# Turning 128-row blocks with VectorE squares of 32 and a DRAM store instead of PE transposes, in a cross-attention and coupled-FFN kernel

## The chip, the cores and the metric

The kernel runs as one program on one NeuronCore of a Trainium2 chip. The time is the device time of one execution in microseconds (us). The engines are named as in the profile: PE (TensorE matmul), PEld (TensorE weight load, which overlaps PE), DVE (VectorE), ACT (ScalarE), POOL (GpSimd) and SP (SyncE, which issues the DMAs here; SPq is its queue). Each engine works through its own instructions in order and waits on semaphores for the others.

## What is computed

`x` is (8, 1024, 512) in fp32, the context is (8, 64, 512). The reference, cut to what matters:

```python
x = x + xattn(layernorm(x), ctx, ctx, Wq, bq, Wk, bk, Wv, bv, Wo, bo, phase)   # 16 heads of 32
x = x + ffn(layernorm(x), ...)

# xattn
qh, kh = rotate(split(q @ Wq.T + bq), phase), rotate(split(k @ Wk.T + bk), phase)
attn = softmax(einsum('bhqd,bhkd->bhqk', qh, kh) / sqrt(32))
return merge(einsum('bhqk,bhkd->bhqd', attn, split(v @ Wv.T + bv))) @ Wo.T + bo

# ffn
gf = global_net(x.mean(axis=1, keepdims=True))
out = x
for _ in range(3):
    tf = sigmoid(gelu(gelu(gelu(out @ w1 + b1) @ w2 + b2) @ w3 + b3) @ w4 + b4)   # 512-512-256-128-1
    coupling = 0.1 + ar * (0.7 * gf + 0.3 * tf - 0.5) * 2.0
    out = out + coupling * twist(out)       # twist: the four quarters of a row, swapped and signed
return out
```

## The kernel before

**The planner.** The body writes nothing to the chip directly. Every call goes through `Engine` (line 304) and becomes an `Op` of a `Plan` (line 127) with an estimated cost (line 334), its dependencies and the buffers it needs. `schedule` (line 225) then plays these operations through as a list scheduler: at each moment every engine takes, of the operations that are ready and whose buffers fit, the one with the lowest priority number. That number is the place in the program plus hand-set offsets by stage (`SHIFT`, `LAST`; `TAIL` from the planned time `FINALE` on). The order found this way is the order in which each engine, and SP's queue of DMAs, runs on the chip. SBUF is cut into rooms: `ROOMS4` = 38 of 4 KB per partition (`r4`) and `ROOMS2` = 16 of 2 KB (`r2`); PSUM has 8 banks. `fits` (line 210) refuses a buffer beyond its tag's cap in `CAPS`, or, for the later operations, into the last `KEEP` rooms while early buffers are still to come.

**The work.** Each of the 8 batches is cut into two halves of 512 rows (`HB`, `TH` = 4 blocks of 128 rows), so there are 16 halves.

The first stretch is attention, half by half. `load_x` (line 472) loads the rows, `ln_stats` (line 680) and `normed` (line 692) form the layer norm, one ACT instruction per block of 128 rows (tile `xna`). The query product needs the 512 features on the partitions, so `turned` (line 704) turns the rows: 16 PE transposes of 128x128 per half into PSUM (`xp_a`), where each bank of 512 columns is then split into a high fp32r part (ACT cast) and a low part (DVE subtraction), `split`, line 438. The product is three fp32r matmuls per pair of blocks (`mm3`, line 428). POOL adds the output bias to the loaded rows meanwhile (line 743). `attn_half` (line 749) then runs the stages `q`, `m` (row maxima), `s` (scores, Exp), `pp` (denominators, which pass through DRAM: `rd`, `rb`), `av`, `o` (output product, added into the rows `xb` and stored as `x2d`) and `ln2`, whose normed rows `xnf` are stored in DRAM as `xnd`, row by row, and added up by POOL (`acc`).

The second stretch is the coupled FFN. A part is a half, except for the last two halves, which are cut into two parts each (`PARTS`). `ffn_load` (line 1019) loads a part's rows from `xnd` (tile `fxn`), and again turns them by PE transposes, 16 per half (`xp_f`), splits them into `fxT`, and forms and splits a sum of two quarters (`fs`). `ffn_part` (line 1048) computes the products K, A and B with first-layer weights that are combined beforehand, and then three cycles of the small network in `rest` (line 1081), in which the later cycles need no new first-layer product. The couplings come back per row through DRAM: `row_of` stores a row, `spread` loads it on all partitions, and `cc` is loaded with one element per descriptor (line 1217). `fin` combines and stores the output.

All GELUs wait for the last Exp (`last_exp`, line 920), and no FFN operation starts before the first PE operation of half `GATE` = 12 (line 931). The turning that the change touches, before:

```python
for t in range(len(piece)):
    with pl.group(also=d):
        pl.tensor.transpose(p[:, ts(t, P)], piece[t][i], ident)
split(d, i, p)
```

Of the kernel before, what the change touches and what calls it, by code (L numbers as in the profile page):

```python
# [22 lines left out]
P = 128  # L23
# [4 lines left out]
ROOMS4, ROOMS2 = 38, 16  # L28
GATE = 12
KEEP = 14  # L30
# [4 lines left out]
CAPS = {'xb': 8, 'wn': 5, 'bv': 1, 'bo': 1, 'jm': 1, 'rt': 1, 'kbd': 2, 'vbd': 2, 'pT': 8, 'acc': 2, 'w3': 3, 'w2f': 1, 'w3f': 1, 'h2': 12, 'w4': 1, 'gw2': 1, 'gw3': 1, 'fxn': 2, 'fs': 5, 'f1': 21, 'AB': 16, 'f2': 7, 'f3': 5, 'c': 12, 'x2': 6, 'xe': 13, 'aT': 6, 'wg': 6, 'w2': 2, 'h1': 8, 'xna': 14, 'xnf': 6, 'xT': 9, 'fxT': 14, 'p': 6, 'sp': 4, 'pp': 2, 'ap': 3, 'op': 2, 'qp': 3, 'xp': 1, 'K': 4, 'A': 6, 'B': 5, 'l2': 6, 'l3': 6, 'l4': 3, 'ct': 3, 'qf': 4, 'qr': 8, 'rb': 4, 'mT': 2, 'mw': 1, 'sT': 8, 'mp': 3, 'dn': 1}  # L35
PARTS = [1, 1, 1, 1, 1, 1, 1, 1, 1, 1, 1, 1, 1, 1, 2, 2]
LAST = {4: -100, 2: -280, 1: -280}
FINALE = 1140
TAIL = {('fin', 4): 354, ('c1', 6): 234, ('load', 3): -490, ('A', 3): -349, ('B', 3): -142, ('c0', 3): -372, ('c1', 3): -209, ('c2', 3): 222, ('fin', 3): -148, ('fin', 6): -215, ('c0', 1): -408, ('fin', 5): 375, ('fin', 1): -152, ('c0', 4): 32, ('load', 6): 78, ('A', 6): 10, ('B', 6): 93, ('c0', 6): -28, ('c2', 6): 61, ('B', 4): 35, ('c0', 2): 110, ('c2', 4): -161, ('c2', 5): 442, ('load', 1): -339, ('A', 1): 40, ('B', 1): 69, ('c1', 1): 114, ('c2', 1): 277, ('A', 2): -131, ('load', 4): 12, ('A', 5): 72, ('load', 5): -177, ('B', 5): 172, ('c0', 5): 88, ('c1', 5): -264, ('fin', 2): 410, ('load', 2): 81, ('c2', 2): 394, ('B', 2): 126, ('c1', 4): 94, ('c1', 2): 29, ('A', 4): -29}
SHIFT = {'ln1': 61, 'q': 194, 'm': 184, 's': -117, 'o': -42, 'pp': -69, 'av': 54, 'ln2': 112, 'load': -267, 'A': -154, 'B': -59, 'c0': -75, 'c1': 114, 'c2': 302, 'fin': -555}  # L40
# [26 lines left out]
class Buf:  # L67


    def __init__(self, make, shape, room=None, tag=None, cap=0):  # L70
        self.make, self.shape, self.room, self.tag, self.cap = make, shape, room, tag, cap
        self.ap = None
        self.writers, self.readers = {}, {}
        self.left = 0
        self.slot = None
        self.counted = False
# [50 lines left out]
class Plan:  # L127


    def __init__(self, tc):  # L130
        self.tc, self.nc, self.ops, self.items = tc, tc.nc, [], None
        self.rooms, self.pools, self.caps = {}, {}, {}
        self.gates, self.stage = [], (None, 0)

        self.late, self.early_bufs, self.keep = False, {}, {}
        for name in ("tensor", "vector", "scalar", "gpsimd", "sync"):
            setattr(self, name, Engine(self, name))
# [33 lines left out]
    def add(self, cost, items, also):  # L171
# [27 lines left out]
        op.late = self.late  # L199
# [10 lines left out]
    def fits(self, op):  # L210
# [4 lines left out]
        for room, bs in need.items():  # L215
            keep = min(op.keep.get(room, 0), self.early_bufs.get(room, 0))
            if len(self.rooms[room]) < len(bs) + keep:
                return False
            for b in bs:
                same = sum(o.tag == b.tag for o in bs)  # L220
                if self.caps[room, b.tag] + same > b.cap:
                    return False
        return True

    def schedule(self):
        ops = self.ops
        for op in ops:
            name, part = op.stage
            op.prio = op.n + SHIFT.get(name, 0) + LAST.get(part, 0)
            op.end_prio = op.prio + TAIL.get((name, part), 0)  # L230
# [5 lines left out]
        while done < len(ops):  # L236
            for e in engines:
# [8 lines left out]
                for o in can:  # L246
# [7 lines left out]
                    saving |= banks >= WIDE  # L254
# [3 lines left out]
                for b in op.bufs:  # L258
                    if b.slot is None:
                        b.slot = self.rooms[b.room].pop(0)  # L260
                        if b.counted:
# [42 lines left out]
class Engine:  # L304
# [3 lines left out]
    def __getattr__(self, method):  # L308
        def call(*args, **kw):
# [19 lines left out]
            issue.turn = method == "transpose"  # L329
# [4 lines left out]
    def cost(self, method, args, kw, outs, reads):  # L334
# [8 lines left out]
        if method == "transpose":  # L343
            return 0.109
# [25 lines left out]
def tile_xattn_ffn(  # L370
# [20 lines left out]
    pl = Plan(tc)  # L391
    pl.room("r4", rm, ROOMS4)
# [79 lines left out]
    def load_x(b, h):  # L472
        xb = []
        for j in range(2):
            t = t4([P, 2, D], "xb", f"xb_{b}_{h}_{j}")
            src = x[b, slice(h * HB + j * 2 * P, h * HB + (j + 1) * 2 * P), :]
            pl.sync.dma_start(out=t, in_=src.rearrange("(t p) d -> p t d", p=P))
            xb.append(t)
        return xb

# [27 lines left out]
    xb0 = load_x(0, 0)  # L508
# [164 lines left out]
    x2d, xnd = {}, {}  # L673
    for b in range(B):
        for h in range(NH):
            for d, nm in ((x2d, "x2d"), (xnd, "xnd")):
                t = dram.tile([P, TH, D], F32, name=f"{nm}_{b}_{h}")
                d[b, h] = pl.fixed(t, [P, TH, D], F32)
# [13 lines left out]
    def normed(src, st, tag, nm):  # L692
        mb, rs = st
        dst = []
        for t in range(TH):
            xn = t2([P, D], tag, f"{tag}_{nm}_{t}")
            pl.scalar.activation(
                xn, src[t // 2][:, t % 2, :], AF.Identity,
                bias=mb[:, t : t + 1], scale=rs[:, t : t + 1],
            )  # L700
            dst.append(xn)
        return dst

    def turned(pieces, tag, nm):


        r = []
        for j, piece in enumerate(pieces):
            w = len(piece) * P
            d = pair4([P, 2, w], tag, f"{tag}_{nm}_{j}")  # L710
            for i in range(2):
                p = bank([P, w], "xp", f"xp_{nm}_{j}{i}")
                for t in range(len(piece)):
                    with pl.group(also=d):
                        pl.tensor.transpose(p[:, ts(t, P)], piece[t][i], ident)
                split(d, i, p)
            r.append(d)
        return r
# [18 lines left out]
    def attn_qx(b, h, xb):  # L737
        nm = f"{b}_{h}"
        stage("ln1")
        xn = normed(xb, ln_stats(xb, f"a{nm}"), "xna", nm)  # L740
        for t in range(TH):
            v = xb[t // 2][:, t % 2, :]
            pl.gpsimd.tensor_tensor(v, v, bo_b, ALU.add)
        return turned(
            [[[xn[t][:, ts(2 * j + i, P)] for i in range(2)] for t in range(TH)] for j in range(2)],
            "xT", f"a{nm}",
        )

    def attn_half(b, h, xb, xnT):
# [49 lines left out]
        for k in range(2):  # L799
# [3 lines left out]
            with pl.group(cost=1.3, also=t):  # L803
# [7 lines left out]
                for g in range(4):  # L811
# [4 lines left out]
                    )  # L816
            for g in range(4):
# [57 lines left out]
        stage("o")  # L875
        for j in range(TH // 2):
# [13 lines left out]
        xn2 = normed(xb, ln_stats(xb, f"f{nm}", ln2[b, h]), "xnf", nm)  # L890
# [3 lines left out]
        acc = accs[b]  # L894
        for t in range(TH):
            pl.sync.dma_start(out=xnd[b, h][:, t, :], in_=xn2[t])
            pl.gpsimd.tensor_tensor(acc, acc, xn2[t], ALU.add)
# [7 lines left out]
    for i, (b, h) in enumerate(halves):  # L905
        starts[i] = len(pl.ops)
        stage()
        xb = load_x(b, h) if i else xb0
        xnT = attn_qx(b, h, xb)
# [9 lines left out]
        attn_half(b, h, xb, xnT)  # L919
# [12 lines left out]
    ORDER = ((4, 5), (2, 1), (0, 3))  # L932
# [4 lines left out]
    def ffn_weights():  # L937
# [3 lines left out]
        pl.vector.tensor_tensor(t[0][:, 0, :], W[2], W[0], ALU.subtract)  # L941
        pl.vector.tensor_tensor(t[0][:, 1, :], W[1], W[3], ALU.subtract)
# [76 lines left out]
    def ffn_load(b, h, t0, n):  # L1019
# [3 lines left out]
        xn = []  # L1023
        for j in range(n // 2):
            t = t4([P, 2, D], "fxn", f"fxn_{nm}_{j}")
            pl.sync.dma_start(out=t, in_=xnd[b, h][:, ts(t0 // 2 + j, 2), :])
            xn.append(t)

        H, L = range(2)
        xT = [two(n * P, "fxT", f"fxT_{nm}_{j}", F32R) for j in range(3)]  # L1030
        for i in range(2):
            s = t2([P, n * P], "fs", f"fs_{nm}_{i}")
            ps2 = []
            for k in (i, i + 2):
                p = bank([P, n * P], "xp", f"xp_f{nm}_{k}")
                j = next(j for j in (1, 2) if k in ORDER[j])
                q = ORDER[j].index(k)
                for t in range(n):
                    with pl.group(also=sum(xT, [])):
                        pl.tensor.transpose(p[:, ts(t, P)], xn[t // 2][:, t % 2, ts(k, P)], ident)  # L1040
                split(xT[j], q, p)
                ps2.append(p)
            pl.scalar.copy(s, ps2[0])
            pl.vector.tensor_tensor(s, ps2[1], s, ALU.add)
            split(xT[0], i, s)
        return xT

    def ffn_part(b, h, t0, n, xT):
# [3 lines left out]
        def product(tag, j, k):  # L1052
# [3 lines left out]
            for c in range(2):  # L1056
                mm3(
                    p, wH[:, c, ts(j, P)], wL[:, c, ts(j, P)], xH[:, c, :], xL[:, c, :],
                    c == 0, c == 1,
# [5 lines left out]
        h1 = two(W, "f1", f"f1_{nm}_0_")  # L1065
        for m in range(NC):
            pl.scalar.copy(Bt[m // 2][:, m % 2, :], product("K", m, 0))
        for m in range(NC):
            j, i = m // 2, m % 2
            p = product("A", m, 1)  # L1070
# [10 lines left out]
        def rest(cyc, h1):  # L1081
# [5 lines left out]
            for j in range(NC // 2):  # L1087
                if not plain:
                    hH, hL = two(W, "h1", f"h1_{nmc}_{j}", F32R)
                    pl.scalar.copy(hH, h1[j])  # L1090
                    low(hL, h1[j], hH)
                for i in range(2):
                    dc = 2 * j + i
                    for m in range(2):
                        if plain:
# [7 lines left out]
                            hH[:, i, :], hL[:, i, :], dc == 0, dc == NC - 1,  # L1103
# [5 lines left out]
            for dc in range(2):  # L1109
# [6 lines left out]
                pl.scalar.copy(hH, f2[:, dc, :])  # L1116
                low(hL, f2[:, dc, :], hH)
                mm3(p, w3p[0][:, dc, :], w3p[1][:, dc, :], hH, hL, dc == 0, dc == 1)
            gelu(f3, p, o3)
            rows = compact and (cyc < CYCLES - 1 or not 0 < part_from_last[0] <= DIRECT2)  # L1120
            if rows:
# [3 lines left out]
                c = small([P, P], "cs", f"c_{nmc}", 4)[: DK * n, :]  # L1125
# [10 lines left out]
            else:  # L1136
# [3 lines left out]
                with pl.group(also=(c,)):  # L1140
                    for t in range(n):
                        pl.tensor.matmul(
                            p[:, t : t + 1], lhsT=f3[:, ts(t, P)], rhs=bcol[:, ow4 : ow4 + 1],
# [46 lines left out]
        if compact:  # L1190
            al, be = (small([P, P], "abs", f"{k}s_{nm}", 4)[: DK * n, :] for k in ("al", "be"))
# [23 lines left out]
        for k, r in enumerate((al_r, be_r)):  # L1215
            with pl.group(cost=(0.5, 4.0)):
                pl.sync.dma_start(out=cc[:, k, :], in_=r.rearrange("o (t p) -> p (o t)", p=P))
# [102 lines left out]
```

## Time and profile before

| | |
|---|---|
| time, median of 3 runs (lowest, highest) | 1298.01 us (1296.53, 1298.63) |
| the profiled execution, its time | 1300.96 us |
| its span in the profile | 1299.1 us |
| mean granted TensorE clock | 0.991 |
| ACT busy | 851.7 us, 1482 instructions |
| POOL busy | 342.4 us, 427 instructions |
| DMA packets, bytes | 111106, 159.07 MB |

The profile is of one execution. Busy time is the time in which an engine had an instruction running; several may overlap, so the mean duration of one instruction times the count can exceed the busy time. A group line reads: engine, operation, output<-input by the program's tile names, shape, count | busy us, mean ns of one | idle time of the engine just before them, and what ended it. All operations have line L326, that of the helper that issues them, so the tile names tell them apart. The PE profile spaces matmuls more closely than their durations: a 128x512 matmul is listed with about 0.39 us and the next one starts 0.23 us later; what a matmul costs on PE's path is the distance from its start to the next one's start.

### The profile page before, as it was taken

To read this page: it belongs to the slowest core of one execution; us is meant where nothing else is said; L and a number is where in the kernel's file an instruction comes from. 1 tells how busy PE (TensorE), PEld (TensorE's weight loads), DVE (VectorE), ACT (ScalarE), POOL (GpSimd) and SP (SyncE) were. 2 spreads that over 40 slices of the span, in tenths; PEclk is the share of its full clock that TensorE was granted. 3 is DMA by queue.
4 is the path that set the end of the run, shared out by engine and by line. 5 is a ranking of instruction groups with operands and counts; after the bars stand their busy time and mean duration, and the time that the engine had idled before them with its cause. 6 is when DMAs were issued, how large, how long until landed. Compare 5 with 4: busy or idle time off the path is not lost. (4 is left out here: it accounts for less than half of the span.)

```text
span 1299.1 us, 21813 instructions
## 1 busy us (share of the span) xinstructions
PE 1264.9 (97%) x8083; PEld 973.9 (75%) x8083; DVE 1067.5 (82%) x1761; ACT 851.7 (66%) x1482; POOL 342.4 (26%) x427
## 2 busy tenths in 40 slices
PE   8999999999999999999999999999999999999995
PEld 7776677666776767666778877788778787789884
DVE  6757887778887878679578988999889898989995
ACT  4663455546455454535467888788787877878886
POOL 3501443424344333322101110111101221001264
PEclk9999999999999999999999999999999999999997
DMA  6313443343434434264213325443244432532444
GB/s 241 108 35 108 159 135 101 128 100 131 109 130 124 148 110 131 99 195 148 96 51 114 101 79 155 150 123 124 79 145 140 152 118 55 171 123 75 133 136 138
DMA packets 111106, 159.07 MB, mean 122 GB/s; under 512 B 33180, under 2 KB 58008, under 8 KB 111000
## 3 DMA queue, kind: packets, MB, share of 16 engines
q1 hardware_dynamic: 111000, 157.69, 38.7%
q8 instruction: 63, 1.03, 0.3%
q14 instruction: 43, 0.35, 0.1%
HBM read 105.62 MB, written 52.03 MB: 121 GB/s over the span
## 5 line engine op out<-in xcount | busy, mean ns | idle before, releaser
L326 PE MATMUL l<-h,w2H 128*128 128x512 f32 (+1 forms) x832 | 247.6, 381 | 2.4 <-ACT h L326 1.2
L326 PEld LDWEIGHTS l<-h,w2H 128*128 128x128 f32 x832 | 148.1, 190 | 32.2 <-issue 4.6
L326 PE MATMUL l<-h,w2L 128*128 128x512 f32 (+1 forms) x416 | 155.0, 373 | 0.0
L326 POOL TENSOR_TENSOR pc<-cc,rs 128x4 f32<-128x4 f32 (+1 forms) x18 | 14.4, 803 | 518.1 <-DMA cc<-ber 515.7
L326 ACT ACTIVATE f<-l,bcol 128x512 f32<-128x512 f32 (+1 forms) x162 | 100.6, 640 | 56.9 <-PE l L326 53.6
L326 DVE TENSOR_TENSOR h<-f,h 128x1024 fp32r<-128x1024 f32 x84 | 102.0, 1218 | 8.2 <-ACT h L326 7.3
L326 POOL TENSOR_TENSOR xb<-xb,bo_b 128x512 f32<-128x512 f32 x64 | 89.8, 1425 | 37.0 <-ACT xna L326 35.4
L326 POOL TENSOR_TENSOR acc<-acc,xnf 128x512 f32<-128x512 f32 x64 | 88.4, 1382 | 37.9 <-ACT xnf L326 34.1
L326 DVE TENSOR_REDUCE mw<-sp 128x8 f32<-128x512 f32 x128 | 82.6, 684 | 14.5 <-PE sp L326 14.3
L326 PEld LDWEIGHTS l<-h,w2L 128*128 128x128 f32 x416 | 79.0, 190 | 14.0
L326 ACT CAST h<-f 128x1024 fp32r<-128x1024 f32 x84 | 87.7, 1053 | 2.5 <-DVE h L326 1.0
L326 ACT ACTIVATE pT<-sT 128x512 f32<-128x512 f32 x128 | 66.2, 602 | 29.5 <-PE sT L326 22.4
L326 ACT ACTIVATE xna<-xb,mb_a,rs_a 128x512 f32<-128x512 f32 x64 | 48.1, 808 | 53.9 <-DVE mb_a L326 45.3
L326 ACT ACTIVATE f<-f,bcol 128x512 f32<-128x512 f32 x112 | 77.6, 727 | 5.0 <-DVE f L326 4.7
L326 ACT ACTIVATE xt<-xt,fa 128x256 f32<-128x256 f32 x128 | 65.0, 591 | 18.0 <-DVE fa L326 17.9
L326 DVE TENSOR_TENSOR xb<-op,xb 128x512 f32<-128x512 f32 x64 | 44.0, 687 | 34.7 <-PE op L326 34.7
L326 ACT ACTIVATE qf<-qp,bqr 128x512 f32<-128x512 f32 x64 | 42.5, 691 | 45.0 <-PE qp L326 44.9
L326 POOL TENSOR_TENSOR rs<-rs,mhalf 128x4 f32<-128x4 f32 x16 | 19.2, 1203 | 189.9 <-DVE rs L326 189.3
L326 DVE TENSOR_TENSOR f<-f,A 128x1024 f32<-128x1024 f32 x56 | 67.8, 1217 | 0.0
L326 ACT ACTIVATE xnf<-xb,mb,rs 128x512 f32<-128x512 f32 x64 | 48.2, 809 | 20.0 <-DVE mb L326 15.8
L326 DVE TENSOR_SCALAR pT<-pT 128x1024 f32<-128x1024 f32 x64 | 45.1, 713 | 19.4 <-ACT pT L326 19.3
L326 POOL TENSOR_TENSOR rs_a<-rs_a,mhalf 128x4 f32<-128x4 f32 x16 | 16.6, 1041 | 152.4 <-DVE rs_a L326 152.4
(402 smaller groups left out, 3646.0 us busy)
## 6 DMA issues: line engine op xcount, KB each, us to landing
xb<-in_x_dram SPq DMA_DIRECT2D x32, 512.0 KB
rb<-rd SPq DMA_DIRECT2D x128, 128.0 KB
x2d<-xb SPq DMA_DIRECT2D x32, 512.0 KB
xnd<-xnf SPq DMA_DIRECT2D x64, 256.0 KB
fxn<-xnd SPq DMA_DIRECT2D x32, 512.0 KB
x<-x2d SPq DMA_DIRECT2D x32, 512.0 KB
xt<-x2d SPq DMA_DIRECT2D x64, 256.0 KB
out_dram<-x SPq DMA_DIRECT2D x32, 512.0 KB
```

The lines of the kernel that those rows point to most:

```text
L326: f(*map(real, args), **{k: real(a) for k, a in kw.items()})
```

## The change

The rows are no longer turned by PE.

For the query product, `load_turned` loads a half's rows so that partition p holds rows 4p to 4p+3 (tile `xa`), the layer norm is written back in place, and the new `turned` lets DVE transpose each pair of blocks in squares of 32x32 into a tile `u` (tag `tn`, 8 KB per partition, one of two rooms `r8`). Four DMAs, one for each 32 partitions, then store `u` to DRAM as rows of the turned matrix (`xtd`); the 512 bytes that belong together are 32 rows times 4. Two DMAs load it back (`xf`), and it is split in pieces of 1024 columns. The rows for the residual are loaded a second time in stage `o`, after the first score product of that half, and POOL's bias addition moves there.

For the FFN, `turned` stores the second layer norm's rows in the same way in `xnd`, and `ffn_load` loads the part's turned matrix and splits it. In the halves of two parts the pieces are 256 bytes and there are eight stores. The columns of a part now stand in the order of (row in block, block), so the per-row couplings `cc` and `c2` are read as `(p t)`.

The planner is altered with it: rooms, caps and offsets are others, `KEEP` goes from 14 to 67, a new rule (`OWED`) keeps rooms of `r4` and `r2` free for operations of up to four units before, `NEAR` gives offsets for the first, the last attention halves and the last three FFN parts, and a wide PSUM group holds banks back only while too few are free. Several groups of operations now claim their output buffers earlier (`also`), and each product A waits for the planned copy of K with the same number.

The diff, cut to its core:

```diff
-ROOMS4, ROOMS2 = 38, 16
+ROOMS8, ROOMS4, ROOMS2 = 2, 35, 14
-KEEP = 14
+KEEP = 67
+OWED = (3, 0)
...
+            if room in ("r4", "r2") and left < OWED[op.late]:
+                owed = sum(self.open[room][max(0, op.unit - 4) : op.unit])
+                if left < min(OWED[op.late], owed):
+                    return False
...
+            op.prio += NEAR.get((name, op.unit), 0)
...
-                    saving |= banks >= WIDE
+                    saving |= banks >= WIDE and banks > len(self.rooms["bank"])
...
+    def load_turned(b, h):
+
+        return load_x(b, h, "xa", "(p t) d -> p t d", t=TH)
...
+    def turned(xn, d, nm, n=TH):
+
+
+        u = pl.tile("r8", [P, NC * NC, TH // n, DK, n], F32, "tn", f"tn_{nm}", ROOMS8)
+        for k in range(TH // 2):
+            to = u[:, :, 2 * k // n, :, 2 * k % n : 2 * k % n + 2]
+            pl.vector.transpose(
+                to.rearrange("p f k t -> p t f k"),
+                xn[k].rearrange("p t (f k) -> p t f k", k=DK),
+            )
+        for i in range(NC):
+            for k in range(TH // n):
+                at = slice((k * P + i * DK) * n, (k * P + i * DK + DK) * n)
+
+                def rows_(a, at=at):
+                    return d[1].rearrange("(f k) t -> k f t", k=DK)[:, :, at]
+
+                with pl.group(cost=(0.6, 2.0)):
+                    pl.sync.dma_start(
+                        out=d[0][:, :, at].via(rows_),
+                        in_=u[ts(i, DK), :, k, :, :].rearrange("p f k t -> p f (k t)"),
+                    )
...
+        normed(xa, xa, ln_stats(xa, f"a{nm}"))
+        turned(xa, xtd[b, h], f"a{nm}")
+        r = []
+        for j in range(2):
+            d = pair4([P, 2, HB], "xT", f"xT_{nm}_{j}")
+            t = t4([P, 2, HB], "xf", f"xf_{nm}_{j}")
+            with pl.group(cost=(1.5, 2.0), also=d):
+                pl.sync.dma_start(out=t, in_=xtd[b, h][0][:, ts(j, 2), :])
+            pl.scalar.copy(d[0], t)
+            low(d[1], t, d[0])
+            r.append(d)
+        return r
...
         stage("o")
+
+        pl.gates.append(scored)
+        xb = load_x(b, h, "xb", "(t p) d -> p t d", p=P)
+        pl.gates.pop()
+        for t in range(TH):
+            v = xb[t // 2][:, t % 2, :]
+            pl.gpsimd.tensor_tensor(v, v, bo_b, ALU.add)
...
+        turned(xn2, xnd[b, h], f"f{nm}", TH // PARTS[NH * b + h])
         for t in range(TH):
-            pl.sync.dma_start(out=xnd[b, h][:, t, :], in_=xn2[t])
-            pl.gpsimd.tensor_tensor(acc, acc, xn2[t], ALU.add)
+            pl.gpsimd.tensor_tensor(acc, acc, xn2[t // 2][:, t % 2, :], ALU.add)
...
-                for t in range(n):
-                    with pl.group(also=sum(xT, [])):
-                        pl.tensor.transpose(p[:, ts(t, P)], xn[t // 2][:, t % 2, ts(k, P)], ident)
-                split(xT[j], q, p)
-                ps2.append(p)
-            pl.scalar.copy(s, ps2[0])
-            pl.vector.tensor_tensor(s, ps2[1], s, ALU.add)
-            split(xT[0], i, s)
+        xf_ = pl.tile("r8", [P, 4, W], F32, "fxn", f"fxn_{nm}", ROOMS8)
+        xf = [xf_[:, ts(j, 2), :] for j in range(2)]
+        for j, q in ((0, slice(1, 3)), (1, slice(0, NC, 3))):
+            with pl.group(cost=(1.5, 2.0), also=sum(xT, [])):
+                pl.sync.dma_start(out=xf[j], in_=xnd[b, h][0][:, q, t0 * P : t0 * P + W])
+            pl.scalar.copy(xT[1 + j][0], xf[j])
+            low(xT[1 + j][1], xf[j], xT[1 + j][0])
+        s = two(W, "fs", f"fs_{nm}_")[0]
         for i in range(2):
+            pl.vector.tensor_tensor(s[:, i, :], xf[1][:, i, :], xf[0][:, 1 - i, :], ALU.add)
+        pl.scalar.copy(xT[0][0], s)
+        low(xT[0][1], s, xT[0][0])
...
-                pl.sync.dma_start(out=cc[:, k, :], in_=r.rearrange("o (t p) -> p (o t)", p=P))
+                pl.sync.dma_start(out=cc[:, k, :], in_=r.rearrange("o (p t) -> p (o t)", p=P))
```

## The prediction

> **What bounds the kernel now.** I read, in this order: the engine totals and the 40 slices, PE's waits, the busy time per half in both stretches, the group lines of what is removed and of what resembles the new work, and PE's and SP's timelines.
>
> ```profile
> span 1299.1 us, 21813 instructions
> PE 1264.9 (97%) x8083; PEld 973.9 (75%) x8083; DVE 1067.5 (82%) x1761; ACT 851.7 (66%) x1482; POOL 342.4 (26%) x427
> PE   8999999999999999999999999999999999999995
> DVE  6757887778887878679578988999889898989995
> ```
>
> PE is busy 97% of the span and idle for 34 us in all, mostly at the two ends. DVE stands second, at 82%. PE's longest waits inside are small:
>
> ```profile
> PE sp L326 <- DVE qr L326: 7.6, 8, 1.4
> PE tr_cT L326 <- DMA c_n<-in_ctx_dram: 6.1, 2, 4.7
> PE l L326 <- DVE h_0L L326: 3.3, 3, 2.5
> ```
>
> (us in total, times, longest.) So PE's own list of instructions is the time, and DVE is what PE waits for where it waits at all. Four windows of busy time, two of attention (one half each, from the first query matmul of a half to the next half's) and two of the FFN:
>
> ```profile
> core 0: us, PE busy (x) PEld busy (x) DVE busy (x) ACT busy (x) POOL busy (x), PEclk, DMA share, GB/s
> 292.40:328.20 35.80, 34.99 (x272) 24.46 (x271) 28.55 (x52) 21.32 (x36) 18.98 (x16) 1.00 0.43 146
> 328.20:361.90 33.70, 33.70 (x270) 24.73 (x269) 26.71 (x49) 14.30 (x25) 9.43 (x6) 1.00 0.40 103
> 830.60:879.10 48.50, 48.50 (x252) 38.14 (x251) 41.66 (x59) 40.26 (x69) 5.13 (x12) 1.00 0.41 131
> 952.70:993.00 40.30, 40.30 (x204) 32.26 (x202) 36.03 (x50) 33.17 (x57) 5.17 (x12) 1.00 0.46 144
> ```
>
> An attention half takes 34.75 us on average of the two, with 27.6 us of DVE (79%); in the FFN DVE stands at 86% to 89% while PE is never idle. PE can thus be kept full beside a DVE at 89%.
>
> **Removed from PE.** 512 transposes: 256 of `xp_a` and 256 of `xp_f`.
>
> ```profile
> L326 PE MATMUL xp_a<-ident,xna 128*128 128x128 f32 x256 | 50.5, 274 | 0.0
> 314.62 1.95 PE L326 MATMUL dn<-pT,dsel 128*32 128x128 f32 x64
> 316.50 0.66 PE L326 MATMUL xp_a<-ident,xna 128*128 128x128 f32 x4
> 316.91 0.48 PE L326 MATMUL qp<-xT_a_1H,wq_1H 128*128 128x512 f32 x1
> 317.23 0.39 PE L326 MATMUL qp<-xT_a_1L,wq_1H 128*128 128x512 f32 x1
> 317.46 0.39 PE L326 MATMUL qp<-xT_a_1H,wq_1L 128*128 128x512 f32 x1
> ```
>
> The listed 274 ns overlap. On the path, four transposes take from 316.50 to 316.91, 0.41 us, and the first matmul after them holds the next back by 0.32 instead of 0.23 us: 0.50 us for a lone group of four. 128 groups of four then cost 128 x 0.41 = 52 us where the switch is paid anyway and 128 x 0.50 = 64 us where each group stands alone. Many stand alone or even in ones and twos; I take 60 us, 30 in each stretch. All of it is on the path, since PE is full around them. No PE instruction is added.
>
> **Moved to DVE.** 2 transposes per turn, 2 turns per half: 64, each 128x1024 fp32 from SBUF to SBUF, written with a step of 16 bytes. No row of before shows this operation. The nearest rows of that size:
>
> ```profile
> L326 DVE TENSOR_TENSOR h<-f,h 128x1024 fp32r<-128x1024 f32 x84 | 102.0, 1218 | 8.2 <-ACT h L326 7.3 <-PE B_3p L326 0.3
> L326 DVE CAST qr<-qf 128x1024 fp32r<-128x1024 f32 x32 | 25.8, 805 | 19.3 <-ACT qf L326 19.1
> L326 DVE RECIPROCAL rc<-dn 128x128 f32<-128x128 f32 x16 | 15.2, 948 | 6.0 <-PE dn L326 6.0
> ```
>
> Below: the cast, 0.81 us. Above: the reciprocal's rate, 948 ns for 128, would make 7.6 us of 1024. The transpose only moves data, which is near the first two; I take the slower of them, 1.22 us: 64 x 1.22 = 78 us. DVE saves where 512-wide low parts from PSUM become 1024-wide ones: for the queries 64 x 0.68 = 43.6 us become 32 x 1.22 = 39; for the FFN 67.6 us (the four `fxT` groups, 38.4 + 19.2 + 6.7 + 3.3) become about 48 x 1.22 = 58.6. Net 78 - 14 = +64: DVE 1131 us.
>
> Beside PE that lies as follows. An attention half has 16 transposes less, 30/16 = 1.9 us: PE's period goes to 32.9. DVE's goes to 27.6 + 4 x 1.22 - 0.3 = 32.2, 98% of it. That looks like a tie, but busy time counts the tails between dependent instructions: four reductions back to back take 2.48 us at 294.40 in DVE's timeline, 0.62 each, where one alone is listed with 0.68. With 9% off, DVE needs about 29.5 of 32.9 us, 90%. An FFN part loses 1.9 us of PE from about 40 and 0.6 of DVE from 36: 93%. So PE remains the bound with less cover; I give 4 us back for DVE waits in attention, none in the FFN. At the lower end, 0.81, that give-back goes; at the upper, 7.6, DVE alone would need 1067 - 14 + 486 = 1539 us.
>
> One rule speaks against this step. The Trainium skill, "SBUF — State Buffer", on SBUF's 16-byte cachelines, wants two hits on a line for full rate, though it calls a step of four fp32 elements free; the transpose's step is just four, and each element it writes lies in a line of its own. No row here has such a write. If the rate halved, the sum by this rule would be about that of the second rival below; by the plain row it is the forecast.
>
> **DMA and SP.** Added: the store of `xtd`, its load and the second load of x, 16 halves x 3 x 1.05 MB = 50 MB.
>
> ```profile
> q1 hardware_dynamic: 111000, 157.69, 38.7%
> ```
>
> By bytes that is 38.7% x 50/157.7 = +12%. By packets: a turn is 2048 pieces of 512 bytes, 32,768 for the queries and 32,768 instead of 8,192 for `xnd`, with 16,000 or so for the loads some 74,000 more, +26% at this mean price. Either way, 51% to 65%, the engines are not full. The one-element packets of `cc` and `c2` shrink to a quarter or half, which I cost at nothing: POOL waits for them off the path. The Trainium skill, "DMA: Bandwidth & Descriptors", Specifications, says that pieces under 512 bytes are read, modified and written. The halves in one part just meet it; the two halves of two parts do not, with 4,096 pieces of 256 bytes each. No row here prices that, and by the rule the last halves' loads would come late and cost a few us.
>
> SP gets 4 + 2 + 2 issues per half more, and 8 for the two cut halves: 136. At the 0.3 to 0.6 us that its timeline shows per issue, about 61 us beside some 300 us of issue time; not a bound. New waits do stand in its queue: the stores wait for DVE, the loads for the stores. Behind them stand `rd` and `rb` (for `av`), `x2d`, and later x loads. The store and load of `c0` show the round trip:
>
> ```profile
> 675.47 0.51 SPq L326 DMA_DIRECT2D c0r<-c  x1
> 677.19 0.33 SPq L326 DMA_DIRECT2D c<-c0r  x1
> 680.34 2.37 DVE L326 TENSOR_TENSOR f<-B,c 128x1024 f32<-128x1024 f32 x2 [0.29 <-DMA c<-c0r]
> ```
>
> 1.72 us from store to the load's issue, 3.15 more to its use. A turn is then 2 x 1.22 on DVE, 4 x 0.45 issues, 1.7 landing, 2 x 0.45 issues, 3.1, and 1.05 + 1.22 for the split: 12 us from normed rows to the operand, where PE did it in 2. The query turn depends on x alone, so it can run a half (33 us) ahead; `xnd` went through DRAM already. I cost both at nothing. If that cover is gone, see the third rival. At the start nothing lies ahead: normed rows of half 0 feed transposes from 33.98 us on, the first query matmul starts at 47.76, and a 12 us turn fits just about; 3 us for that.
>
> The second load of x is released a score product early and needed at `o`; the whole of `av` lies between, so nothing. ACT loses the PSUM copies of `fs` and half of its cast starts, some 30 us off the path. The planner's new numbers I cannot price; -10 to +10 us for the order's luck, zero taken.
>
> **Sum.** Profiled execution 1300.96 (span 1299.1 and 1.9 around it) - 60 (PE) + 4 (DVE waits) + 3 (start) = 1248. The median is 2.95 below the profiled execution, so 1245; with the transposes at 64 instead of 60 it is 1241. I say 1243. Own range: 52 to 64 us of PE, 0 to 15 of waits, 10 either way for the order; all low ends together give 1298 - 64 + 3 - 10 = 1227, and all high ends but the order's 1298 - 52 + 15 + 3 = 1264.
>
> **Rivals.** Second: DVE becomes attention's bound. With t per transpose a half needs 27.3 + 4t of DVE; it reaches the old period of 34.75 at t = 1.86 us. The attention gain is then gone and the FFN's 30 us remain: 1298 - 30 = 1268. For it: 98% by plain busy time, and the unknown write step. Against it: the 0.62 us back to back, and that only one operand is read.
>
> Third, on the slower side: the turn through DRAM is not ahead, because the two 8 KB rooms and SP's order hold it back until shortly before its use. Its place is before the query product. If half of its 12 us show in each half, 16 x 6 = 96 us against 60 gained: 1298 - 60 + 96 = 1334. It decides from 60/16 = 3.75 us shown per half. For it: SP waits in order, and each turn needs a room until its stores have landed. Against it: a room is held some 6 us twice per 33 us, and PE has the previous half's `sT`, `dn`, `ap` and `op` to do.
>
> Fourth: transposes were filler in gaps that stay, and the order gives nothing: 1298. Against it: PE idles 0.8 us or less in the two attention windows, which leaves no such gaps. Fifth: the freed bank and the new order also win back some of the 34 idle us: 1218.
>
> **How the numbers follow.** Forecast 0.66; DVE-bound attention 0.15; turn exposed 0.10; nothing 0.03; order wins more 0.06. Two per mille, 2.6 us, is about what a measurement of this kernel tells from no change. Faster takes the first, second and fifth: 0.87; same 0.03; slower 0.10. The range reaches from the fifth's side, 1222, into the second, 1274; left out are the third and fourth and the tails, about 2 in 10.
>
> **What would show it.** No `xp` groups, PE busy near 1205 us and idle under 45. DVE near 1130 us, its transposes near 1.2 us; above 1.9 the second rival holds. PE's waits on `xT` for the query product, near zero if the turn is ahead. Wrong altogether if PE's busy time does not fall by 50 us, or if DVE's or DMA's waits on PE grow by more than it falls.

## The result and the profile after

The changed kernel takes 1352.55 us (median of 4 runs, 1348.44 to 1357.01), the kernel before 1298.32 us beside it: ratio 1.0421, 95% interval 1.0386 to 1.0456. It is slower by 54.6 us; the forecast was 1243. In what follows a difference to the kernel before is always (ratio - 1) x 1298 us, since the runs of before differ by 1 to 2 us from chip to chip.

The top of the page after, to be read against the lines of before in the prediction (engine totals, then busy tenths of PE, DVE and of the DMA engines in 40 slices, then the DMA queue):

```profile
span 1346.7 us, 20903 instructions
PE 1245.6 (92%) x7571; PEld 931.6 (69%) x7571; DVE 1168.6 (87%) x1739; ACT 828.5 (62%) x1360; POOL 343.8 (26%) x427
...
PE   8889888988999999998899999999999999989984
...
DVE  7699989988998898888978998699889899697895
...
DMA  6677778686866555556521432334253333441354
...
q1 hardware_dynamic: 175704, 208.03, 51.1%
```

PE has 512 instructions less, but its busy time fell by 19 us, not 60, and it is now idle for 101 us (span minus busy) instead of 34. Part of this is the granted clock, 0.973 after and 0.991 before: (1 - 0.973) x 1347 = 36 us of full clock are missing over the span, against (1 - 0.991) x 1299 = 12. An estimate from these figures is that the lower clock accounts for at most 25 us of the loss; it was not measured by itself, and it stands inside the costs found below rather than beside them, since PE's idle stretches come with them. DVE gained 101 us, not 64. The DMA share of the span came out at 51.1%, as forecast by bytes; the slices show what that mean hides: 6 to 8 tenths in the first half of the span, 3 to 4 in the second.

The new operation, from the groups by line:

```profile
L343 DVE STREAM_TRANSPOSE tn_a<-xa 128x1024 f32<-128x1024 f32 x32 | 64.6, 2033 | 0.5 <-ACT xa L343 0.3
L343 DVE STREAM_TRANSPOSE tn_f<-xnf 128x1024 f32<-128x1024 f32 x32 | 62.4, 1968 | 4.8 <-ACT xnf L343 4.5
```

2.03 and 1.97 us each, against 1.22 in the forecast and 1.86, from which on the second rival was to hold. The busy times per stretch of the attention, of after and of before:

```profile
core 0: us, PE busy (x) PEld busy (x) DVE busy (x) ACT busy (x) POOL busy (x), PEclk, DMA share, GB/s
60.00:150.00 90.00, 79.35 (x596) 52.00 (x596) 83.89 (x131) 48.29 (x74) 21.84 (x18) 0.94 0.76 224
150.00:300.00 150.00, 134.04 (x927) 90.81 (x928) 140.27 (x217) 71.39 (x108) 63.71 (x45) 0.98 0.74 215
300.00:450.00 150.00, 139.07 (x1027) 93.61 (x1025) 136.24 (x202) 72.73 (x110) 54.55 (x41) 0.98 0.67 193
```

```profile
60.00:150.00 90.00, 90.00 (x730) 64.93 (x729) 63.91 (x109) 43.06 (x72) 21.90 (x17) 1.00 0.27 82
150.00:300.00 150.00, 147.43 (x1162) 103.73 (x1160) 118.34 (x211) 79.04 (x129) 63.47 (x50) 1.00 0.43 128
300.00:450.00 150.00, 148.34 (x1135) 106.77 (x1127) 122.04 (x221) 75.10 (x123) 57.03 (x44) 1.00 0.40 121
```

In attention DVE is now the fuller engine (140 of 150 us) and the DMA engines carry 215 instead of 128 GB/s. PE's waits, the longest first and then those on the turned operand:

```profile
PE l L343 <- ACT h_0H L343: 10.4, 5, 5.4
PE mp L343 <- DVE mw L343: 7.6, 15, 1.8
PE dn L343 <- DVE pT L343: 7.3, 5, 3.6
PE sp L343 <- DVE qr L343: 6.9, 7, 2.1
...
PE qp L343 <- ACT xT_1H L343: 2.7, 2, 1.5
PE qp L343 <- DVE xT_1L L343: 2.0, 3, 0.8
```

The query turn runs ahead as forecast: PE waits for it 4.7 us in all. It waits for the rest of the attention's DVE work instead (`mw`, `pT`, `qr`). By the traces' start and end times of the named products:

| us | last output product (`op`) ends | first `A` of the FFN starts | end | from first `A` to end |
|---|---|---|---|---|
| before | 642 | 595 | 1299 | 705 |
| after | 666 | 645 | 1347 | 702 |

So there are two things to explain: attention lost 24 us (by its last product) to 50 us (by the FFN's first) where it should have gained 30, and the FFN, which has none of the query turn's DMAs and only the last two of the 64 transposes on its DVE, gained 3 us where it should have gained 30.

### The profile page after: what moved, and what is told of

It reads as the page before. It is cut to its first block, busy times and chain, and to the rows that moved or that the text cites. A ratio compares the mean times of both kernels' runs of the same rounds, so it can differ in the third digit from the quotient of the medians.

```text
span 1346.7 us, 20903 instructions
## 1 busy us (share of the span) xinstructions
PE 1245.6 (92%) x7571; PEld 931.6 (69%) x7571; DVE 1168.6 (87%) x1739; ACT 828.5 (62%) x1360; POOL 343.8 (26%) x427
## 3 DMA queue, kind: packets, MB, share of 16 engines
q1 hardware_dynamic: 175704, 208.03, 51.1%
## 5 line engine op out<-in xcount | busy, mean ns | idle before, releaser
L343 PEld LDWEIGHTS l<-h,w2H 128*128 128x128 f32 x832 | 151.8, 191 | 43.5 <-DVE h L343 11.3
L343 POOL TENSOR_TENSOR xb<-xb,bo_b 128x512 f32<-128x512 f32 x64 | 97.2, 1549 | 178.0 <-DMA xb<-in_x_dram 115.6
L343 POOL TENSOR_TENSOR pc<-cc,rs 128x4 f32<-128x4 f32 (+1 forms) x18 | 11.4, 634 | 442.1 <-DMA cc<-ber 307.3
L343 ACT ACTIVATE xa<-xa,mb_a,rs_a 128x512 f32<-128x512 f32 x64 | 47.7, 807 | 42.5 <-DVE mb_a L343 40.4
L343 DVE STREAM_TRANSPOSE tn_f<-xnf 128x1024 f32<-128x1024 f32 x32 | 62.4, 1968 | 4.8 <-ACT xnf L343 4.5
L343 DVE STREAM_TRANSPOSE tn_a<-xa 128x1024 f32<-128x1024 f32 x32 | 64.6, 2033 | 0.5 <-ACT xa L343 0.3
L343 ACT CAST xT_1H<-xf 128x1024 fp32r<-128x1024 f32 x16 | 16.8, 1048 | 64.7 <-DMA xf<-xtd 64.7
```

Source lines behind the costliest of these rows:

```text
L343: f(*map(real, args), **{k: real(a) for k, a in kw.items()})
```

## The experiments

In all of them each engine runs the same list in the same order as the kernel they come from (after, or before); only what an instruction does or moves is changed, or whether it is issued at all. The exceptions are the doubled transposes of e12 and DMAs that are added or cut in two.

**e1, dense writes.** The transposes write their 1024 elements one after another instead of with a step of four; the DMAs stay, so rows land in a scrambled order.

```diff
-            to = u[:, :, 2 * k // n, :, 2 * k % n : 2 * k % n + 2]
+            flat = u.rearrange("p f q k t -> p (f q k t)")[:, ts(k, 2 * D)]
+            to = flat.rearrange("p (t f k) -> p t f k", t=2, k=DK)
```

> The changed kernel with its order of instructions unchanged; DVE's transposes write their squares one after the other in SBUF (a step of 4 bytes) instead of with a step of 16 bytes, so the turned rows are arranged wrongly, while stores, loads and all else move the same bytes. Theory 1 (the write step makes a transpose 2.03 us instead of 1.2, and DVE is attention's bound): transposes near 1.2 us, DVE busy falls by 64 x 0.8 = 51 us, most of it on the path, time 1295 to 1310. Theory 2 (the turn through DRAM and its 512-byte pieces is late): 1340 to 1355 although the transposes are shorter. Theory 3 (the planned order itself is bad, whatever a transpose costs): also 1335 to 1355.

1337.04 us, ratio 1.0306 (1.0275 to 1.0336), and a transpose now takes 1231 ns. The write step costs 0.80 us of 2.03 per transpose and 15 us of the 54.6 by itself.

**e3, copies.** The same with a plain copy in place of each transpose.

> The changed kernel in the same order with a plain DVE copy of 128x1024 in place of each transpose, so that the rows are not turned. Theory 1: a copy takes 0.6 to 0.8 us, DVE falls by 64 x 1.3 = 83 us; if DVE still bound attention with 1.2 us, the time falls further than with dense writes, to 1270 to 1290; if not, it stays within 5 us of that run. Theories 2 and 3: 1335 to 1355.

1333.41 us, 1.0278 (1.0249 to 1.0306). A copy of `xa` takes 0.80 us, of `xnf` 1.24, where the dense transposes of e1 take 1.23 each. Moving the data is most of a dense transpose, and 4 us separate the two kernels, within their intervals.

**e2 and e9, a step of two elements, all rows in place.** If a half's rows are dealt in pairs, the transpose writes two adjacent elements (step 8 bytes). In e2 the load of x does the dealing:

```diff
+        src = x[b, ts(h, HB), :].rearrange("(i j k t) d -> j i k (t d)", i=NC, j=2, t=2)
```

> The same computation as the changed kernel, the same order and the same 512-byte stores; rows are loaded so that each transpose writes its pairs of rows side by side, with a step of 8 bytes. Theory 1: as the transposes of the two cut halves, which have this step and take 1.2 us; time 1295 to 1310. Theories 2 and 3: 1335 to 1355. If the step must be 4 bytes for the full rate, transposes stay near 2.0 us and the time near 1350.

1440.79 us, 1.1121 (1.1077 to 1.1164), though its transposes take 1.24 us. DVE's waits for the loaded rows show why, in e2 and then in after:

```profile
DVE st_a L343 <- DMA xa<-in_x_dram: 77.2, 17, 11.2
...
DVE st_a L343 <- DMA xa<-in_x_dram: 6.8, 6, 3.3
```

The load's outermost dimension is 4 here. The Trainium skill, "DMA: Bandwidth & Descriptors", section "Why a DMA increments its semaphore by 16 and not by 1", says that a DMA is spread over the largest number of engines up to 16 that divides its outermost dimensions, which makes four of this one; this run shows the late loads but not the engines. e9 keeps 128 partitions outermost, loads 4 KB runs and lets PE read the moving operand in the dealt order:

```diff
+            t = t4([P, 2, D], "xa", f"xa_{b}_{h}_{j}")
+            r = slice(h * HB + j * 2 * P, h * HB + (j + 1) * 2 * P)
+            pl.sync.dma_start(out=t, in_=x[b, r, :].rearrange("(p t) d -> p t d", t=2))
...
+        return v.via(lambda a: a.rearrange("p (i q w) -> p q i w", i=NC, q=2))
```

> The same computation as the changed kernel, in the same order and with the same stores: x is again loaded in whole runs of 4 KB per partition, DVE writes pairs side by side (a step of 8 bytes), and PE reads the columns of its moving operand in blocks of 64 to put them in natural order. Theory 1: transposes at 1.2 us as in the two cut halves, and a time like that of the run with dense writes, 1333 to 1342. If it stands near 1440 as the earlier run with pairs did, it was not the load of x in that run that cost 100 us. Theory 3 adds nothing here: the rest over 1298 stays.

1334.59 us, 1.0268 (1.0215 to 1.0320). The line of its query transposes (those of the FFN take 1237 ns):

```profile
L343 DVE STREAM_TRANSPOSE tn_a<-xa 128x1024 f32<-128x1024 f32 x32 | 39.5, 1234 | 0.6 <-ACT xa L343 0.5
```

So the load carries the e2 loss: all of it lies in attention (from first `A` to end e2 takes 702 us and e9 703), and the small loads of the couplings, which differ too, belong to the FFN. Two adjacent elements per write are as fast as dense ones, and the whole change with that repair is still 35 us slower than before.

**e4, bigger pieces.** The stores of the turn leave 8 KB in one piece instead of 16 of 512 bytes (the turned rows land in another order).

```diff
+                    return d[1].rearrange("(i k f) t -> i k (f t)", i=NC, k=DK)[at.start // P]
```

> The changed kernel in the same order and with its transposes as they are, but each store of a turn writes one run of 8 KB per partition instead of sixteen pieces of 512 bytes, so the turned rows stand in other places in DRAM. Theory 2 (small pieces load the DMA engines so that turns and other transfers come late): DMA share in attention falls from 0.7 towards 0.6, time 1300 to 1330. Theories 1 and 3: 1345 to 1355, unchanged.

1338.87 us, 1.0320 (1.0283 to 1.0356): 13 us of the loss go with the pieces, at the same bytes, with 118,104 packets instead of 175,704. The DMA share did not fall as expected: 0.76 from 150 to 300 us and 0.64 from 300 to 450, after 0.74 and 0.67.

**e5 and e6, a light turn.** e5 stores and loads only a fraction of the query turn's bytes; e6 in addition loads an eighth of the second x.

```diff
+                f = 1 if i and nm[0] == "a" else NC * NC
+                cut = lambda a, f=f: a[:, 0:f, :]
...
+                part = lambda a: a[:, :, 0:64]
+                pl.sync.dma_start(out=t.via(part), in_=xtd[b, h][0][:, ts(j, 2), :].via(part))
```

> The changed kernel in the same order of instructions; the query turn's stores and loads move 0.4 MB per half instead of 2 MB (pieces are left out, the same number of DMAs is issued, and the split reads one loaded eighth of the columns over and over, so the query product is not the reference's). Theory 2 in the form that is left (the added bytes crowd the DMA engines in attention): DMA share from 0.75 to below 0.6, time falls by more than 12 us, to 1320 or 1335. Theory 3 (the planned order leaves the removed PE time idle): 1342 to 1355.

> As the run before, and the second load of x also moves an eighth of its bytes (the residual rows are replaced by the bias), so that the DMA bytes are about those of the kernel before. Theory 2: 1310 to 1325, with POOL's waits for the second load mostly gone. Theory 3: 1340 to 1355.

1332.58 us, 1.0275 (1.0225 to 1.0324), and 1330.79 us, 1.0261 (1.0162 to 1.0360). The turn's traffic costs 19 us; e5 takes off 26 MB and 23,040 packets, so bytes and pieces are not told apart, and it issues as many DMAs as after, so these 19 us are not SP's issue time. For the second x no cost shows, but the two runs of e6 lie 10 us apart, so a few us would not be seen. In e6 DVE is busy 146.49 of the 150 us from 150 to 300, with the DMA share at 0.56.

**e7, both.** e6 and e1 together.

> As the run before, with dense writes of the transposes too: what is left over the forecast's 1243 is then neither the write step nor the bytes. If these two were all, 1245 to 1265; if the planned order keeps the gain from showing (its own plan ends only 5 us before that of the kernel before), 1290 to 1310.

1303.94 us (8 runs), 1.0065 (1.0040 to 1.0090). Against after: e1 alone -15, e6 alone -21, together -46. That looks as if each hid a part of the other, but e6 is known to 13 us only, so the 10 us beyond the sum are not shown.

**e8, the traffic alone.** The kernel before with three more stores of each `xb` tile, 50 MB.

```diff
+                for k in range(3):
+                    more = dram.tile([P, 2, D], F32, name=f"more_{nm}_{j}{k}")
+                    pl.sync.dma_start(out=pl.fixed(more, [P, 2, D], F32), in_=xb[j])
```

> The kernel before in its own order, with three further stores of each half-load of rows to spare DRAM, 3 MB a half, 50 MB in all, spread over attention. Theory 2: slower by 15 us or more. Theory 3: within 4 us of the kernel before.

1319.96 us, 1.0178 (1.0135 to 1.0221): 23 us, all before the FFN (the last `op` ends at 663 instead of 642, the first `A` starts at 617 instead of 595). Bytes and 96 issues on SP were added here, nothing else, and the DMA engines were not full (columns as above):

```profile
150.00:300.00 150.00, 146.44 (x1105) 102.96 (x1104) 114.48 (x205) 74.22 (x121) 59.61 (x46) 1.00 0.61 206
300.00:450.00 150.00, 147.88 (x1141) 103.47 (x1141) 117.75 (x212) 73.20 (x121) 58.98 (x46) 1.00 0.65 221
```

Of PE's waits, the one on the rows of the FFN (`fxn`, loaded from DRAM) grew most, from 0.3 to 6.2 us. What carries the rest of the 23 us stays open.

**e10, before without its transposes.** The order of before; the 512 PE transposes are not issued, and the splits read a constant tile.

```diff
+                        to.skip = True
...
-                split(d, i, p)
+                split(d, i, still(p, w))
```

> The kernel before in its own order with its 512 PE transposes not issued; the copies and subtractions after them are issued as before but read a constant, so the rows are not turned. It measures the 60 us of the sum by themselves. If freed PE time shows in an order made for it elsewhere filled (the forecast's step): 1234 to 1246. Theory 3 (with the transposes gone, chains through ACT and DVE set the time in the FFN and the tail): 1265 to 1295, with PE idle risen by what is missing.

1284.39 us, 0.9904 (0.9884 to 0.9924): 12.5 us, not 60. One thing clouds it: the low parts of the queries' operand took 1031 and 815 ns from the constant instead of 680. In e11 they take 677 and 676.

**e11 and e12, a quarter and twice.** e11 issues one transpose of each group and the splits read its 128 columns in the bank again and again; e12 issues every transpose twice.

```diff
+                        to.skip = t > 0
...
+        return p.via(lambda a: a[:, :P].rearrange("p (o k) -> p o k", o=1).to_broadcast([P, w // P, P]))
```

```diff
+                if kw.get("out") is None and outs and getattr(outs[0], "twice", False):
+                    f(*map(real, args), **{k: real(a) for k, a in kw.items()})
```

> The kernel before in its own order; of each group of PE transposes only the first is issued, 128 of 512, and the split reads its 128 columns of the bank again and again, still from PSUM and still waiting for PE. 384 transposes are left out, three quarters of the forecast's 60 us. If PE's list is the time, as the forecast had it: 1298 - 45 = 1253. If the transposes filled gaps that chains through DVE and ACT leave (now the leading theory): 1284 to 1292, PE's idle time up by some 25 us and the waits sp<-DVE qr and l<-DVE h longer. If the 12.6 us of the run without transposes were spoilt by low parts that took longer from the constant, this one, whose low parts read PSUM as before, comes out faster than that run's 1284.

> The kernel before in its own order with each of the 512 PE transposes issued twice; nothing else changes. If PE's list is the time, +60 us by the forecast's 0.117 each: 1358; by the 0.109 us that they are spaced by, +56: 1354. If they lie in gaps: much less, 1305 to 1325. In between, 1325 to 1345, it would mean that gaps are few but the freed time of PE can't be used, because the next operand isn't there earlier.

e11 1281.01 us, 0.9880 (0.9862 to 0.9897): 15.6 us of the 45. e12 1345.28 us, 1.0373 (1.0357 to 1.0389): 48 us of the 56. The totals of e11, then of e12:

```profile
span 1278.3 us, 21068 instructions
PE 1234.0 (97%) x7707; PEld 930.2 (73%) x7707; DVE 1064.8 (83%) x1761; ACT 848.6 (66%) x1482; POOL 340.6 (27%) x427
```

```profile
span 1342.6 us, 22837 instructions
PE 1314.7 (98%) x8595; PEld 1028.0 (77%) x8595; DVE 1070.4 (80%) x1761; ACT 857.2 (64%) x1482; POOL 351.5 (26%) x427
```

The transposes do not lie in gaps, or doubling them would have been cheap. By e12 one costs 48/512 = 0.095 us, which makes 36 us for the 384 of e11 and 48 for the 512 of e10; taking them away returned 15.6 and 12.5. So PE's list sets the time when work is added to it, and something else does almost at once when work is taken from it. The busy share hides this: PE is 97% busy in before and in e11 alike, and its idle time rose by 10 us only, not by the 25 expected. The starts of PE's instructions show where the freed time went. Counted from each start to the next, the transposes take 43.0 us in before and 9.6 in e11, 33 less, while the products `l` of the small network take 7 more, `qp` 3 and `sT` 3; in e10 the 43.0 go, and `l` and `qp` take 9 more each and `sT` 6.

**e13, after with everything light.** e7 with the transposes cut to an eighth of their elements.

```diff
-            flat = u.rearrange("p f q k t -> p (f q k t)")[:, ts(k, 2 * D)]
+            flat = u.rearrange("p f q k t -> p (f q k t)")[:, ts(k, P)]
```

> The kernel after, in its own order, with the light turn and the dense writes of e7 and the 64 DVE transposes cut to an eighth of their elements (128x128 instead of 128x1024): some 64 us of DVE time less than e7. If the new order itself holds PE back, it stays near e7's 1304: 1295 to 1304. If DVE's time for the transposes is what is left, it comes to the 1284 of before without its PE transposes, or below; the forecast's PE term would give 1243 to 1250 here, since neither DVE nor DMA costs anything any more.

1293.22 us (10 runs), 0.9969 (0.9950 to 0.9987): 12 us below e7, 4 below before, and 8.5 above e10, whose DVE time is about the same (1086.6 here, 1079.9 there). The two differ in the order, but not in it alone: e13 still turns the FFN's rows through DRAM (152,664 packets against 111,000) and ran at a clock of 0.981 against 0.992. From first `A` to end it takes 705 us.

**e14 and e15, is it DVE that stands behind PE?** DVE computes the low parts of the queries' and the FFN's operands for 128 columns only, and PE reads these in place of the rest: e14 in before, e15 in e11.

```diff
+            pl.vector.tensor_tensor(cut(d[1][:, i, :]), cut(full), cut(f32(d[0][:, i, :])), ALU.subtract)
...
+                        xH[:, dc % 2, :], again(xL[:, dc % 2, :]), dc == 0, dc == NC - 1, also=(d,),
```

> The kernel before in its own order with all its PE transposes; VectorE computes the low parts of the query's and the FFN's operands for the first 128 columns only, and PE reads these again and again in place of the rest: some 60 to 75 us of DVE time less, no PE work less. If PE's list alone sets the time, PE's waits of some 10 us at most can go: 1287 to 1298. If DVE and PE bind together, it gains more, 1265 to 1285, as PE's waits shrink and its stretched matmuls with them.

> e11 (one transpose in four) and e14 (cut low parts) together. If e11 gained 15 us of its 45 because DVE stands right behind PE, the two together gain clearly more than the sum of the two alone: 1250 to 1262, the forecast's 45 us. If what stops PE in e11 is neither of them (order, chains through ACT), the two only add up, or less: above 1265.

e14 1291.87 us, 0.9954 (0.9939 to 0.9968); e15 1267.06 us, 0.9759 (0.9741 to 0.9777). The totals of e15:

```profile
span 1265.8 us, 21055 instructions
PE 1225.8 (97%) x7707; PEld 931.7 (74%) x7707; DVE 1009.1 (80%) x1761; ACT 847.0 (67%) x1482; POOL 349.5 (28%) x427
```

Alone, 384 transposes less give 15.6 us and 55 us of DVE less give 6.0, the latter inside the range that e14 was given for PE's list alone; together they give 31.3, which is 9.7 more than the sum, known to about 4. So DVE's work on these low parts is one of the things right behind PE. That rests on this excess and not on the ranges: 1267 lies above the 1250 to 1262 that this theory asked for, but the sum of the two alone would be 1276. It is not all: with the low parts cut, the 384 transposes give 25 us (e15 against e14), where e12's price makes 36 and the forecast's 45. What holds the rest was not settled; PE's waits that grew point at the chain through ACT as well as DVE, first two lines of e15 and then one of before, where the wait on `qr` was 7.6 us:

```profile
PE sp L328 <- DVE qr L328: 11.0, 11, 1.5
...
PE l L328 <- ACT f L328: 4.8, 10, 1.6
...
PE l L326 <- ACT f L326: 2.6, 4, 1.6
```

Two things were not measured: the change for the FFN alone, and an order made with the transposes' true durations.

## Why the prediction was wrong

Taking the change apart from its end gives the account, against before: after +54.6; light turn and second x (e6) +33.9; dense writes too (e7) +8.4; transposes nearly gone too (e13) -4.0. The forecast stood at -55, and its PE term alone at -60. Taken off in this order, the traffic costs 21 us, the write step 26 and the transposes' own time 12; the first two are known to some 13 us each, since e6 is, and in the other order the write step comes to 15 (e1). The rest, some 55 us, is a gain that never came.

- **Failed, the largest: "All of it is on the path, since PE is full around them", with "PE can thus be kept full beside a DVE at 89%".** PE 97% busy says that adding to PE costs (e12: 48 us for 512, 0.095 us each, so the price of 0.117 was also a quarter too high). It does not say that taking work from PE gains. What stood behind was not priced: DVE's instructions, at 79 to 89%, and by the waits alone also their chains with ACT. Measured: -12.5 for all 512 (e10), -15.6 for 384 (e11), and -25 for 384 once DVE has 55 us less to do (e15 against e14). The comparison of an FFN part, "93%. So PE remains the bound", was a comparison of mean shares; from first `A` to end the FFN went from 705 to 697 us in e11, where 75% of 30 would have been 22; in e15 it went to 686, of which the cut low parts alone (e14) make 8.
- **Failed in size: the transpose at 1.22 us.** It measured 2.03 and 1.97 us; 64 of them are 127 us, not 78. The second rival named the right point (1.86 us) and cause, the unknown write step. Its 1268 kept the FFN's 30 us, which were not there, and counted only DVE. The measured times are 2.03 us with one element in every 16 bytes (after), 1.234 with two adjacent ones (e9) and 1.231 with four (e1). That agrees with the Trainium skill, "SBUF — State Buffer", Specifications (TRN2), which asks for two hits on a 16-byte line for full rate. The same page's note on cachelines, in the section "Door 1: The DMA port swizzle", calls a step of four fp32 elements free; for this instruction the measurement says otherwise.
- **Failed: DMA at nothing, "Either way, 51% to 65%, the engines are not full".** The share was right (51.1%), the conclusion not. The 50 MB fall into the first 600 us, where the share is 0.67 to 0.76 from 60 to 450 us and 0.57 after that. Put on before alone, 50 MB cost 23 us (e8); taking 26 or 41 MB off after gave 19 and 21 (e5, e6), and bigger pieces at the same bytes gave 13 (e4). Why traffic costs time below full engines was not settled. The rule of the Trainium skill, "DMA: Bandwidth & Descriptors", Specifications, that pieces under 512 bytes are read, modified and written was not priced by itself: in the trace after, packets of 256 bytes took 17.7 ns on average and those of 512 bytes 31.8, which is a tenth more per byte.
- **The order at zero:** e13 lies 8.5 us above e10, within the 10 allowed for it. What is left of the FFN's turn and the lower clock are in that number too, so the order's own part is not known.
- **Right:** the query turn runs ahead (4.7 us of PE waits on it), so the third rival, which names 1334, fell although the time lies on its side; 3 us for the start (first query matmul at 50 us instead of 48). That the second load of x costs nothing fits (e6 against e5: 2 us less), but the interval of e6 leaves room for several us.
- **The fourth rival** was dismissed because "PE idles 0.8 us or less in the two attention windows, which leaves no such gaps". e12 shows that dismissal to be right about gaps, and e10 shows its consequence to be wrong: most of the time saved stays away all the same. No case in the list was the one that came: costs of the transposes, of their write step and of the traffic, each thought covered, on top of a gain of which the next bound takes most.

## What to carry to other kernels

A full engine tells what work added to it costs; what work taken from it gains is told by the second engine and the chains behind it, and leaving the work out in the old order is the test that prices it (here 12.5 us, where the forecast had 60 and adding the same work cost 48). Read the DMA share in the stretch where the bytes fall, not over the span. When two costs are found in one stretch, remove them together as well as one by one: here they gave 15 and 21 us alone and 46 together, though the noise of one run leaves open whether that is more than the sum.

## What the runs showed of the hardware

- The VectorE transpose of 128x1024 fp32 in SBUF takes 1.23 us with dense writes or a step of 8 bytes, and 2.03 us with a step of 16 bytes; a plain copy of the same tiles takes 0.80 and 1.24 us.
- 50 MB more in the first 600 us cost 23 us while the DMA engines' share was still 0.61 to 0.65 (e8); PE's idle time grew from 34 to 46 us over the span.
- A load whose outermost dimension is 4 made the same bytes cost some 110 us more than one with 128 partitions outermost (e2 against e9, by their ratios), all of them in attention.
- The granted clock fell mostly where PE idled: from 60 to 80 us PE was busy 14.23 of 20 us after, at a clock of 0.74, and 20.00 of 20 before, at 1.00. It is no firm rule here: from 160 to 180 us PE was busy 16.92 of 20 us after, at a clock of 1.00. The mean over the span went from 0.991 to 0.973. How much of the loss this makes was not measured by itself; by the estimate above it is at most 25 us.
